# One matmul a unit later, and one load a tile later, in a two-layer attention kernel

## The chip, the cores and the metric

The kernel runs on one core of a Trainium2 chip. The metric is the device time of one execution in microseconds; the time before is 2504.33 us, the median of 3 runs (2504.14 to 2504.37). All arrays are f32.

A core has engines that run side by side, each through its own list of instructions in order, and that wait for one another by semaphores: TensorE (PE) multiplies matrices into PSUM, VectorE (DVE), ScalarE (ACT) and GpSimd (POOL) work elementwise, and SyncE (SP) issues most DMAs here.

## The reference

Four images of 128 channels by 64x64 pixels, so 4 batches of 4096 tokens of 128 channels, go through two layers. Cut to what matters:

```python
# layer 0: group norm, attention over all 4096 tokens, residual
xn = gn(x); q = Wq xn + bq; k = Wk xn + bk; v = Wv xn + bv      # q, k: 64 channels
x = x + v softmax(q^T k)^T
# layer 1: layer norm, causal attention with 128 channels, residual
t = tokens(x); n = ln(t)
t = t + softmax(mask(n Wq^T (n Wk^T)^T / sqrt(128))) (n Wv^T)
# recurrent feed-forward: layer norm, matrix, batch norm over all tokens, residual
w = bn(ln(t) W^T); y_i = sigmoid(w_i + y_{i-1} V^T); t = t + y
```

## The kernel before, in words

Work is cut into tiles of 512 queries (c = 0 to 7), in order of batch (b), layer, tile. A tile runs through its keys in units (u) of 2 x 128 keys: 16 units for each tile of layer 0, 2(c+1) units for tile c of layer 1, which is causal. The main loop emits, for each unit i, `score(i)`, one `step()` of side work, and `product(i-1)`.

`score` multiplies keys with queries into PSUM (L1090 in layer 0, L1083 in layer 1; tile `ps`) and ScalarE takes the exponential into `s`, one of three buffers (L1092, L1096). In layer 1 GpSimd masks the blocks on the diagonal (L1099). `product` adds `s` into `total` on VectorE (L1126, L1131) and multiplies it with the values into `av` in PSUM (L1134). In layer 1 the "values" are the normalised tokens themselves; the matrix of values W1v is applied to the finished tile instead.

When a tile has seen its last unit, a generator `finish` is made, and each `step()` advances it by one `yield`: VectorE sums `total` (L949 to L953), makes the reciprocal of the row sums (L957 to L964), and scales `av` to `o` (L966). Then `project` follows. In layer 0 it adds `o` to X (L975) and ends. In layer 1 it lets a number of steps pass (`waits`), multiplies `o` with W1v on TensorE (`po`, L981) and adds it to X, which gives `X2` (L984). When it is done, the feed-forward's part for this tile (`ffn`) enters the list of side work: the tile is stored (`kept`), turned to tokens by a transpose on VectorE (L758), a write to DRAM and four reads back (L760, L765, all on SP), and its statistics are taken (L740).

The side work beside layer 1 includes the keys of the next batch's layer 0: `xg` (normalised input, L681, after which GpSimd adds a bias to X, L683), `pk` (L686), `K` (L707, L708), and the values `pv` (L715, ScalarE's copy L716). In batch 0 these have no earlier layer to hide beside and run in the first tile of layer 0: the keys of block k are needed by unit 2k.

`load_x(b)` issues eight DMAs of 256 KB for one batch's input, on SP. For batch 1 it is called in `product`, with a small tile of `total` as `behind`: GpSimd first writes one column of each eighth of X from it (L505), and the DMAs, which overwrite those, wait for that. The statistics of batch 1 (`gn_stats`, L649: eight of 512 columns, then L653) are put into the side work when tile 2 of layer 0 begins. The order of instructions on each engine is not quite the order of emission: a scheduler with its own estimate of times sets it, except in stretches marked `manual_schedule`.

Of the kernel before, what the change touches and what calls it, by code (L numbers as in the profile page):

```python
# [32 lines left out]
QT = 512  # L33
# [441 lines left out]
def fast_kernel(  # L475
# [12 lines left out]
    NQ = N // QT  # L488
# [12 lines left out]
    def load_x(b, behind=None):  # L501

        X[b] = xpool.tile([P, N], F32, tag=f"X{b % 2}", name=f"X{b}")
        if behind is not None:
            nc.gpsimd.tensor_copy(X[b].rearrange("p (h n) -> p h n", h=8)[:, :, 0], behind)  # L505
        for h in range(8):
            eng = nc.scalar if b == 0 and h % 2 else nc.sync
            eng.dma_start(out=X[b][:, ts(h, N // 8)], in_=x[b, :, ts(h, N // 8)])
# [87 lines left out]
    with ExitStack() as actx:  # L596
# [10 lines left out]
        def misc(name):  # L607
            return ps_m.tile([P, QT], F32, tag="m", name=name)
# [335 lines left out]
        def finish(b, layer, c, off, w, av, total):  # L944

            name = f"{layer}_{b}_{c}_{off}"
            k = w // 32
            t = tmp.tile([P, QT], F32, tag="a", name=f"t_{name}")[:, :w]
            nc.vector.tensor_tensor(t, total[:, 0, :w], total[:, 1, :w], ALU.add)  # L949
            tt = tmp.tile([P, QT], F32, tag="b", name=f"tt_{name}")[:, :w]  # L950
            nc.vector.transpose(tt, t)  # L951
            part = small.tile([P, 16], F32, tag="part", name=f"part_{name}")
            nc.vector.tensor_reduce(part[:, :k], tt.rearrange("p (k j) -> p k j", j=32), AX.X, ALU.add)  # L953
            yield
            side = small.tile([32, 4, 16], F32, tag="side", name=f"side_{name}")
            for q in range(4):
                nc.vector.tensor_copy(side[:, q, :k], part[ds(32 * q, 32), :k])  # L957
            z = small.tile([P, 16], F32, tag="z", name=f"z_{name}")
            nc.vector.tensor_reduce(z[0:32, :k], side[:, :, :k].rearrange("j q k -> j k q"), AX.X, ALU.add)
            nc.vector.reciprocal(z[0:32, :k], z[0:32, :k])  # L960
            for q in range(1, 4):
                nc.vector.tensor_copy(z[ds(32 * q, 32), :k], z[0:32, :k])
            rb = tmp.tile([P, 16, 32], F32, tag="a", name=f"rb_{name}")[:, :k, :]
            nc.vector.transpose(rb, z[:, :k].unsqueeze(2).to_broadcast([P, k, 32]))  # L964
            o = tmp.tile([P, QT], F32, tag="b", name=f"o_{name}")[:, :w]
            nc.vector.scalar_tensor_tensor(  # L966
                o, rb.rearrange("p k j -> p (k j)"), GUARD, av[:, :w], ALU.mult, ALU.mult
            )
            yield from project(b, layer, c, off, w, o, 5 if w < QT else 3 if c == NQ - 1 else 2)

        def project(b, layer, c, off, w, o, waits):
            cols = ds(c * QT + off, w)
            xt = X[b][:, cols]
            if layer == 0:
                nc.vector.scalar_tensor_tensor(xt, o, 1.0 / GUARD, xt, ALU.mult, ALU.add)  # L975
                yield
                return
            for _ in range(waits):
                yield
            po = misc(f"po_{b}_{c}_{off}")[:, :w]  # L980
            nc.tensor.matmul(po, lhsT=W1v, rhs=o, start=True, stop=True)  # L981
            if c == 0:
                X2[b] = xpool.tile([P, N], F32, tag="X2", name=f"X2_{b}")
            nc.vector.scalar_tensor_tensor(X2[b][:, cols], po, 1.0 / GUARD, xt, ALU.mult, ALU.add)  # L984
            yield
# [17 lines left out]
        def whole(key):  # L1003
            for _ in made[key]:
                pass
            done(key)
# [98 lines left out]
        def product(i):  # L1105
            b, layer, c, off, w, u, n = units[i]
            d = st[b, layer, c, off]
            s, first = scores.pop(i)
            if u == 0:
                d["av"] = ps_av.tile([P, QT], F32, tag="av", name=f"av_{i}")  # L1110
                d["total"] = acc.tile([P, 2, QT], F32, tag="total", name=f"total_{i}")
            av, total = d["av"], d["total"]
            both = first[0] == first[-1]
            last = i == len(units) - 1
            if last:

                pz = misc("pz_last")
                for h in range(2):
                    nc.tensor.matmul(pz[:, 0:1], lhsT=total[:, h, :w], rhs=ones[:, 0:1], start=h == 0, stop=False)
            halves = (slice(0, len(first)),) if both else range(2)  # L1120
            if u == 0:
                if not both:
                    nc.vector.memset(total[:, 1, : first[1]], 0.0)
                for h in halves:
                    f = first[0] if both else first[h]
                    nc.vector.tensor_copy(total[:, h, f:w], s[:, h, f:w])  # L1126
            elif not last:
                for h in halves:
                    f = first[0] if both else first[h]
                    t = total[:, h, f:w]  # L1130
                    nc.vector.tensor_tensor(t, t, s[:, h, f:w], ALU.add)  # L1131
            V = V1[b] if layer else V0[b]
            for h in range(len(first)):
                nc.tensor.matmul(  # L1134
                    av[:, first[h] : w], lhsT=V[:, 2 * u + h, :], rhs=s[:, h, first[h] : w],
                    start=u == 0 and h == 0, stop=2 * u + h == n - 1,
                )
            if (b, layer, c, u) == (0, 0, 0, 4):
                load_x(1, total[:, 0, 0:8])
            if last:  # L1140
                for h in range(2):
                    nc.tensor.matmul(pz[:, 0:1], lhsT=s[:, h, :w], rhs=ones[:, 0:1], start=False, stop=h == 1)
                return av, pz, s
            if 2 * u + len(first) == n:
                for key in list(ends):
                    whole(key)
                key = ("e", b, layer, c, off, w)
                made[key] = finish(b, layer, c, off, w, av, total)
                ends.append(key)
# [25 lines left out]
        for i in range(len(units) + 1):  # L1175
            if i < len(units):
                score(i)
            if i:
                step()
                ended = product(i - 1)  # L1180
# [8 lines left out]
    with ExitStack() as fctx:  # L1189
# [94 lines left out]
        for n in range(1, len(steps[2])):  # L1284
# [15 lines left out]
            elif n >= last and late and WARM + late[0][1] + late[0][2] <= n:  # L1300
                b, l, k = late.pop(0)
# [76 lines left out]
```

## Time and profile before

| | |
|---|---|
| median of runs | 2504.33 us |
| the profiled execution: its time, its span | 2503.85 us, 2502.1 us |
| PE, DVE, ACT, POOL busy | 2466.4, 1778.1, 1137.5, 206.9 us |
| products `av`, layer 0 (L1134) | 2048 matmul instructions, 592 ns each with overlap |
| scores `ps`, layer 0 (L1090) | 2048, 492 ns |
| sums `total` (L1131) | 809 on VectorE, 882.5 us |
| granted TensorE clock | 0.998 |

In the profile's lines, a row of a group reads: line, engine, operation, output<-input, shape, count, then busy time and the mean of one. A row in order of time reads: start and duration in us, engine, line, operation, output<-input, shape and count, and in brackets the idle time of the engine before it and what ended it. A row of waits reads: who waited for whom, then total us, times, and the longest. Each f32 matmul of the program shows as two instructions, and matmuls overlap, so the distance from one start to the next says more than a duration.

### The profile page before, as it was taken

How to read it: one execution, taken by the hardware profiler on the slowest of the kernel's cores; microseconds unless marked ns; L12 is line 12 of the kernel's file. 1: busy time of each engine (PE TensorE's matmuls, PEld its weight loads, DVE VectorE, ACT ScalarE, POOL GpSimd, SP SyncE). 2: the span in 40 equal slices, each digit the busy share in tenths (PEclk: the TensorE clock that was granted, in tenths of full speed). 3: DMA queues.
4: the chain of work that ended last, by engine and by line, in shares of the span. 5: the costliest groups of instructions: out<-in, count | busy, mean ns of one | idle time of the engine just before them, and what ended most of it. 6: DMA issues, size and time to landing. Idle time of an engine off the chain costs nothing.

```text
span 2502.1 us, 22482 instructions
## 1 busy us (share of the span) xinstructions
PE 2466.4 (99%) x7345; PEld 1339.4 (54%) x7345; DVE 1778.1 (71%) x3571; ACT 1137.5 (45%) x1422; POOL 206.9 (8%) x281
## 2 busy tenths in 40 slices
PE   7999999999999999999999999999999999999997
PEld 4555554444555555444555555544455555544465
DVE  7776669655977667856687676876578676786667
ACT  4444444454444444445444444454444444434456
POOL 2010001210000100110000010121010000010000
PEclk9999999999999999999999999999999999999999
DMA  2000001100100000100010000101010000010023
GB/s 75 9 17 9 17 9 41 27 17 13 51 13 9 17 9 18 39 25 13 22 46 13 13 9 18 34 26 26 13 47 17 9 14 12 9 34 17 9 74 138
DMA packets 154078, 64.40 MB, mean 26 GB/s; under 512 B 136160, under 2 KB 136928, under 8 KB 152160
## 3 DMA queue, kind: packets, MB, share of 16 engines
q1 hardware_dynamic: 151344, 59.27, 8.9%
q10 hardware_dynamic: 2608, 3.61, 0.4%
q8 instruction: 60, 0.98, 0.2%
q14 instruction: 66, 0.54, 0.1%
HBM read 31.66 MB, written 31.20 MB: 25 GB/s over the span
## 4 chain that ended last, share of the span: by engine, by line
PE 94%; DVE 3%; ACT 2%; issue 1%; POOL 0%; DVEq 0%; POOLq 0%; ACTq 0%
PE av L1134 52%; PE ps L1090 19%; PE ps L1083 17%; PE po L981 1%; PE pw_f L841 1%; PE pq L804 1%; PE pv L715 1%; PE pk L686 1%; ACT WX L1234 1%; DVE total L1131 1%; ACT states L1234 0%; PE pz L1233 0%; ACT WXp L1234 0%; ACT s L1092 0%; DVE stats L649 0%
## 5 line engine op out<-in xcount | busy, mean ns | idle before, releaser
L1131 DVE TENSOR_TENSOR total<-total,s 128x1024 f32<-128x1024 f32 (+5 forms) x809 | 882.5, 1094 | 539.6 <-ACT s L1092 290.9
L1134 PE MATMUL av<-s,WXp 128*128 128x512 f32 x2048 | 962.1, 592 | 0.0
L1092 ACT ACTIVATE s<-ps,shift 128x1024 f32<-128x1024 f32 x512 | 569.6, 1114 | 760.4 <-PE ps L1090 743.5
L1090 PE MATMUL ps<-q,K 128*128 128x512 f32 x2048 | 757.5, 492 | 1.7 <-DVE K L708 1.5
L1096 ACT ACTIVATE s<-ps,zero,R 128x512 f32<-128x512 f32 (+3 forms) x607 | 405.3, 718 | 513.6 <-PE ps L1083 506.5
L1134 PEld LDWEIGHTS av<-s,WXp 128*128 128x128 f32 x2048 | 384.7, 188 | 303.6 <-issue 263.1
L1090 PEld LDWEIGHTS ps<-q,K 128*128 128x128 f32 x2048 | 386.0, 189 | 290.4 <-issue 230.7
L1134 PE MATMUL av<-s,V 128*128 128x512 f32 (+3 forms) x1214 | 504.3, 538 | 0.0
L1083 PE MATMUL ps<-q,X 128*128 128x512 f32 (+3 forms) x1214 | 503.5, 537 | 0.0
L1083 PEld LDWEIGHTS ps<-q,X 128*128 128x128 f32 x1214 | 225.1, 190 | 236.1 <-issue 219.4
L1134 PEld LDWEIGHTS av<-s,V 128*128 128x128 f32 x1214 | 223.9, 190 | 229.2 <-issue 205.7
L579 POOL TENSOR_TENSOR rstd<-rstd,mhalf 128x4 f32<-128x4 f32 x32 | 32.4, 1011 | 1024.2 <-DVE rstd L578 1024.2
L1099 POOL TENSOR_SCALAR_AFFINE_SELECT s<-s 128x128 f32<-128x128 f32 x128 | 49.0, 387 | 532.8 <-ACT s L1096 531.7
L579 POOL TENSOR_TENSOR rstd_f<-rstd_f,mhalf 128x4 f32<-128x4 f32 (+1 forms) x32 | 47.3, 1480 | 383.1 <-DVE rstd_f L578 362.6
L683 POOL TENSOR_SCALAR X<-X,B0v 128x512 f32<-128x512 f32 x32 | 64.5, 2019 | 139.8 <-DVE xg L681 138.3
L796 DVE TENSOR_SCALAR V<-V,lmv,rstd 128x128 f32<-128x128 f32 x128 | 38.6, 344 | 37.0 <-POOL rstd L579 36.9
L729 DVE TENSOR_TENSOR q<-QR,qh 64x512 fp32r<-64x512 f32 x64 | 44.0, 688 | 6.8 <-PE ps L1090 5.5
L949 DVE TENSOR_TENSOR t<-total 128x512 f32<-128x512 f32 x64 | 44.0, 688 | 4.3 <-PE pfw L638 2.5
L951 DVE STREAM_TRANSPOSE tt<-t 128x512 f32<-128x512 f32 x64 | 45.2, 706 | 1.8
L964 DVE STREAM_TRANSPOSE rb<-z 128x512 f32<-128x512 f32 x64 | 44.8, 700 | 0.9
L966 DVE SCALAR_TENSOR_TENSOR o<-rb,av 128x512 f32<-128x512 f32 x64 | 43.6, 681 | 2.4
L957 DVE COPY side<-part 32x16 f32<-32x16 f32 (+1 forms) x256 | 41.3, 161 | 3.9
(191 smaller groups left out, 1227.8 us busy)
## 6 DMA issues: line engine op xcount, KB each, us to landing
turn<-t SPq DMA_DIRECT2D x32, 256.0 KB, 2.0
V<-turn SPq DMA_DIRECT2D x128, 64.0 KB, 2.5
turn_f<-t_f SPq DMA_DIRECT2D x31, 256.0 KB, 2.0
t_f<-turn_f SPq DMA_DIRECT2D x124, 64.0 KB, 2.5
X<-in_x SPq DMA_DIRECT2D x28, 256.0 KB, 4.5
kept<-X SPq DMA_DIRECT2D x24, 256.0 KB, 2.0
Y<-kept SPq DMA_DIRECT2D x6, 1024.0 KB, 8.3
out<-Y SPq DMA_DIRECT2D x5, 1024.0 KB, 6.0
```

Source lines behind the costliest of these rows:

```text
L579: nc.gpsimd.tensor_tensor(dst, dst, mhalf[:, :n], ALU.pow)
L683: nc.gpsimd.tensor_scalar(xt, xt, B0v, None, ALU.add)
L729: nc.vector.tensor_tensor(q[ds((1 - h) * CQ, CQ), h, :], src, high[rows, :], ALU.subtract)
L951: nc.vector.transpose(tt, t)
L964: nc.vector.transpose(rb, z[:, :k].unsqueeze(2).to_broadcast([P, k, 32]))
L1083: nc.tensor.matmul(ps[:, h, first[h] : w], lhsT=lhsT, rhs=q[:, off + first[h] : off + w], start=True, stop=True,)
L1090: nc.tensor.matmul(ps[:, h, :], lhsT=lhsT, rhs=q[:, k, :], start=k == 0, stop=k == 1)
L1092: nc.scalar.activation(s, ps, AF.Exp, bias=shift)
L1096: nc.scalar.activation(part, ps[:, h, first[h] : w], AF.Exp, scale=scale, bias=zero)
L1099: nc.gpsimd.affine_select(out=edge, in_=edge, pattern=[[1, P]], base=0, channel_multiplier=-1, compare_op=ALU.is_ge, fill=0.0,)
L1131: nc.vector.tensor_tensor(t, t, s[:, h, f:w], ALU.add)
L1134: nc.tensor.matmul(av[:, first[h] : w], lhsT=V[:, 2 * u + h, :], rhs=s[:, h, first[h] : w], start=u == 0 and h == 0, stop=2 * u + h == n - 1,)
```

## The change

```diff
@@ finish
-            yield from project(b, layer, c, off, w, o, 5 if w < QT else 3 if c == NQ - 1 else 2)
+            yield from project(b, layer, c, off, w, o, 5 if w < QT else 3 if c in (1, NQ - 1) else 2)
@@ product
-            if (b, layer, c, u) == (0, 0, 0, 4):
+            if (b, layer, c, u) == (0, 0, 1, 4):
                 load_x(1, total[:, 0, 0:8])
```

The first edit lets one more step pass before `po` of tile 1 of layer 1, in each of the four batches. That tile's ending runs during tile 2, which has six units. The second edit calls the load of batch 1 sixteen units later, in tile 1 of layer 0 instead of tile 0. The statistics of batch 1 are still put into the side work at tile 2. Shapes, sizes and the number of matmuls and DMAs stay.

## The prediction

> **What bounds the kernel now.** I read the busy shares first, then the waits of TensorE, then its instructions in order of time at the two places that the change touches.
>
> ```profile
> span 2502.1 us, 22482 instructions
> PE 2466.4 (99%) x7345; PEld 1339.4 (54%) x7345; DVE 1778.1 (71%) x3571; ACT 1137.5 (45%) x1422; POOL 206.9 (8%) x281
> ```
>
> PE is busy for 99% of the span. The change adds and removes no matmul, so it can move the time only through gaps on PE. The waits of PE:
>
> ```profile
> PE pg L657 <- DVE mv L653: 10.6, 1, 10.6
> PE rest L1326 <- DVE good L1324: 5.1, 1, 5.1
> PE po L981 <- DVE o L966: 2.2, 3, 0.7
> PE pk L686 <- DVE xg L681: 1.7, 1, 1.7
> PE ps L1090 <- DVE K L708: 1.5, 3, 0.6
> ```
>
> 10.6 is the first load and 5.1 the closing check; the change touches neither, nor the 1.7 before the first keys. Left are `po` (2.2 us, three times) and `ps` behind `K` (1.5, three times). The ends of matmuls are modelled, so I measure both from start to start. First `po`, in batch 0:
>
> ```profile
> 404.75 1.88 PE L1134 MATMUL av<-s,V 128*128 128x512 f32 x4
> 406.47 1.67 PE L1083 MATMUL ps<-q,X 128*128 128x512 f32 x4
> 408.88 1.12 PE L981 MATMUL po<-o,W1v 128*128 128x512 f32 x2 [0.74 <-DVE o L966]
> 409.84 1.05 PE L715 MATMUL pv<-W0v,xg 128*128 128x128 f32 x8
> ```
>
> The same group of four scores (two 512, two 384 wide) took 1.50 us at 385.85. It therefore ended at 407.97, but `po` began at 408.88: 0.91 lost. From `po` to `pv` it is 0.96, against 0.86 for the unstalled `po` at 393.80: 0.10 more. In batch 1 (score group at 1008.04, `po` at 1010.43) the loss is 0.89+0.10, in batch 2 (1609.58, 1611.99) 0.91+0.11; the `po` of batch 3 at 2197.3 has no key matmuls around it and waits for nothing. Sum 3.0 us.
>
> The second place is the first tile, with two units to each block of 512 keys:
>
> ```profile
> 46.08 1.88 PE L1134 MATMUL av<-s,WXp 128*128 128x512 f32 x4
> 48.55 2.09 PE L1090 MATMUL ps<-q,K 128*128 128x512 f32 x8 [0.59 <-DVE K L708]
> ...
> 53.94 1.88 PE L1134 MATMUL av<-s,WXp 128*128 128x512 f32 x4
> 56.10 2.08 PE L1090 MATMUL ps<-q,K 128*128 128x512 f32 x8 [0.28 <-DVE K L708]
> ```
>
> Four `av` passes take 1.72 us (58.88 to 60.60, a turn without a wait), so `ps` could have begun at 47.80 and 55.66: lost 0.75 and 0.44. Likewise 0.20 before 40.69 and 0.31 before 70.55, nothing before 63.07. Sum 1.7 us. Why `K` is late, on VectorE:
>
> ```profile
> 58.45 2.56 DVE L1131 TENSOR_TENSOR total<-total,s 128x1024 f32<-128x1024 f32 x2 [2.50 <-ACT s L1092]
> 61.02 0.74 DVE L697 TENSOR_SCALAR QR<-pk,B0qk 64x512 f32<-64x512 f32 x1
> 61.78 0.42 DVE L707 TENSOR_SCALAR kh<-k 64x512 int32<-64x512 int32 x1
> 62.24 0.69 DVE L708 TENSOR_TENSOR K<-k,kh 64x512 fp32r<-64x512 f32 x1
> ```
>
> This is an undisturbed turn: K ends at 62.93 and `ps` starts at 63.07 (0.14 later), just in time. In the turns before, the eight L649 statistics of batch 1 (5.1 us of VectorE between 20 and 72) stand in this queue. All that PE can still win here is 3.0+1.7 = 4.7 us.
>
> [...] `pv` waited at 409.84 behind `po` with its own input long there. [...] beside batch 2's load a turn's write at 647.46 was read back only from 651.64 (4.2 us; at 94.38 it took 2.0). [...] the statistics here take 0.66 to 0.70 us with a load beside them or without.
>
> **The change, part by part.** I use the order of instructions on each engine that the built kernel has.
>
> 1. `po` of the second tile goes behind `pv` (8 passes, 0.89), the next `av` (1.72) and the narrow scores (0.65). PE then asks for `o` at 407.97+3.26 = 411.2; `o` began at 408.14 and took 0.69, so it is 2.4 us early. Gain 0.91+0.10 in each of three batches: **-3.0**. What is late next: X2 (L984) now waits for `po` at 412.1 instead of 409.8 and, in VectorE's queue, for the narrow sum of a GpSimd-masked score. That mask stands behind GpSimd's 1.57 us on X; xg at about 412.5 gives the masked score at 415.2, while PE wants it for `av` at 416.2: 1.0 us to spare. X2 then comes near 416, the transpose near 417.3 (414.49 before), its turn is back near 424, and its statistics stand behind a sum near 428. The FFN's own DMAs (one kept copy, one write, four reads on SP) move with it by under 3 us and nothing else waits on SP there. Cost 0; without that cover I would price the wait at 1.0 us a batch.
>
> 2. In the first tile the eight statistics and their aggregate (8 x 0.64 + 0.37 = 5.5 us of VectorE) leave. But the order on PE moves too: for four pairs the even unit's `ps` now stands before the last `av` product, 0.86 us earlier, and the odd one after it. I work out that loop. From the even `ps` (0) the odd one starts at 0.93+0.86 = 1.79; its exponential 1.21 later (83.11 to 84.32), 3.00, ends 4.11; the sum (1.23) ends 5.34; QR to the end of K 1.91 (61.02 to 62.93) and 0.14 to PE: 7.40. PE's own work in a turn is 1.86+0.86+1.72+0.89+1.72 = 7.05. So K is still 0.35 late in a turn. The first such `ps`: without the statistic of 0.69, K ends at 39.81, start 39.95. Three turns of 7.40 give 62.15; the last pair, not split, is PE's: 62.15+7.05+0.86 = 70.06, against 70.55. Gain **-0.5**. Ends: -1.7 if every wait goes, +0.5 if each of four turns loses 0.25 more than I count.
>
> 3. In the second tile the load's mark on GpSimd comes after the sum at 88.62 to 89.85; SP issues at 90.2 (0.2 after, as at 35.35 to 35.58) and eight issues of 0.43 end at 93.9, ahead of the turn's transpose. GpSimd is idle from 57 to 106 and SP from 39 to 94, so nothing is queued there. VectorE reaches the first statistic after X at 93.65; the first piece lands about 4.2 after its issue (646.13 to 650.32), 94.4: a wait of 0.8. With statistics and transpose between them, the sums of the next units end up to 2.7 us late. That is covered: three score buffers and 2.65 us a unit mean that a sum may be 7.94-1.11-1.23 = 5.6 us late before an exponential waits. The turn's write at 95 shares the engines with the load (36 to 43.3 before, so until 98), is read back near 104, and its reader, now behind another sum, comes at 107.8. Cost 0. A precedent is batch 2's load:
>
> ```profile
> 647.50 1.23 DVE L1131 TENSOR_TENSOR total<-total,s 128x1024 f32<-128x1024 f32 x1
> 650.32 1.36 DVE L649 BATCH_NORM_STATS2 stats<-X 128x6 f32<-128x512 f32 x2 [1.58 <-DMA X<-in_x]
> ```
>
> VectorE stood 1.58 us there and the scores on PE went on at 647.47, 650.12 and 652.76, one unit of 2.65 apart.
>
> Sum -3.0-0.5 = -3.5. The profiled execution took 2503.85 (span 2502.1 and 1.75 around it), so 2500.35; the median of runs is 0.48 above it: **2500.8 us**. Measurement tells about 0.2% (5.0 us) from no change, so this counts as same.
>
> **Rivals.** (a) All waits go: K is in time because VectorE runs ahead. For it: 63.07 shows a turn without loss; against it: the earlier `ps`. 2504.33-4.7 = 2499.6. (b) The first tile gains nothing or loses up to 0.5, as the earlier `ps` waits as long as the statistics did: 2501.3 to 2501.8. (c) `po`'s wait only moves: the masked score or a PSUM buffer holds PE 1.0 us in each batch. Against it: the 1.0 us to spare and the two buffers concerned, freed by q at 401.8 and by X2 at 400.6. 2503.8. (d) Slower: VectorE, in order, stands before the first statistic until the load lands, and sums and score buffers behind it stop ScalarE and then PE. It costs from a landing 2.9 us later than I count (5.6-2.7), 1 us for 1 us, and decides from 6.4 us, where it eats the 3.5; 8.5 us would be needed beyond that start for +5.0. Pieces landed within 6.7 us of issue, 2.5 later than 4.2, so it does not begin. A landing 9 us later gives 6.1-3.5 = +2.6, 2507. That the edit moves nothing is excluded by the built order for (1) and (2).
>
> **How the numbers follow.** My forecast 0.60, (a) 0.12, (b) 0.14, (c) 0.07, (d) 0.07. Range: the forecast with the ends of step 2 is 2499.6 to 2501.8; to leave out no more than 2 in 10 and allow for part of (c), 2499.4 to 2502.8. Faster than 2499.3 would need more than all the waits I found: 0.04. Slower by over 5.0 is the worse part of (d): 0.05. Same 0.91.
>
> **What would show it.** Right: no `po` in the list of PE's waits; `pv` directly after the 384-wide scores; no wait of 0.7 at any `ps` in the first tile, small ones of 0.3 at most; VectorE waiting about 1 us for X in the second tile; units 2.65 us apart there. Wrong: a new wait of PE on GpSimd's masked score near 415, units stretched between 90 and 110, or `K` waits as large as before.

## The result, and the profile after

The changed kernel takes 2500.82 us (median of 22 runs, 2500.48 to 2501.77); the kernel before took 2504.70 beside it (2503.66 to 2505.83). The ratio is 0.9985, with a 95% interval of 0.9979 to 0.9990: 3.9 us, or 0.16%. The interval lies below 1, but the difference is smaller than the 0.2% up to which it counts as no change. Where 3.9 us went can't be read from run times; the traces have to say it. The page of the changed kernel (profiled execution 2500.77 us):

```profile
span 2499.0 us, 22485 instructions
PE 2465.6 (99%) x7345; PEld 1338.1 (54%) x7345; DVE 1777.2 (71%) x3571; ACT 1137.3 (46%) x1422; POOL 211.3 (8%) x281
```

The same 7345 matmuls, and the span is 3.1 us shorter. Its waits of PE (who waited for whom, total us, times, longest):

```profile
PE pg L657 <- DVE mv L653: 10.7, 1, 10.7
PE rest L1326 <- DVE good L1324: 5.2, 1, 5.2
PE pk L686 <- DVE xg L681: 1.7, 1, 1.7
PE ps L1090 <- DVE K L708: 1.4, 4, 0.7
```

The line of `po` is gone; that of `K` stays almost as it was (1.4 against 1.5; one wait of each list, 0.7 here and 0.6 before, belongs to the very first keys, near 20 us, which the change doesn't touch). PE in order of time around `po` in batch 0:

```profile
406.42 1.67 PE L1083 MATMUL ps<-q,X 128*128 128x512 f32 x4
407.93 1.05 PE L715 MATMUL pv<-W0v,xg 128*128 128x128 f32 x8
408.82 1.88 PE L1134 MATMUL av<-s,V 128*128 128x512 f32 x4
410.54 0.82 PE L1083 MATMUL ps<-q,X 128*128 128x256 f32 x4
411.19 1.02 PE L981 MATMUL po<-o,W1v 128*128 128x512 f32 x2
```

The score group starts at 406.42, and 1.51 later `pv` follows, which is that group's own 1.50. `po` comes at 411.19, and the next row is 0.86 behind it. No stall is left. In the first tile, on PE:

```profile
46.29 1.02 PE L1134 MATMUL av<-s,WXp 128*128 128x512 f32 x2
47.52 1.17 PE L1090 MATMUL ps<-q,K 128*128 128x512 f32 x4 [0.21 <-DVE K L708]
...
53.78 1.02 PE L1134 MATMUL av<-s,WXp 128*128 128x512 f32 x2
55.01 1.16 PE L1090 MATMUL ps<-q,K 128*128 128x512 f32 x4 [0.21 <-DVE K L708]
```

Two `av` passes are 0.86 from start to start, so `ps` could have begun at 47.15 and 54.64: 0.37 lost in each turn, and a turn is 55.01-47.52 = 7.49. VectorE in one of those turns:

```profile
44.23 1.23 DVE L1131 TENSOR_TENSOR total<-total,s 128x1024 f32<-128x1024 f32 x1 [0.56 <-ACT s L1092]
45.47 0.74 DVE L697 TENSOR_SCALAR QR<-pk,B0qk 64x512 f32<-64x512 f32 x1
46.23 0.42 DVE L707 TENSOR_SCALAR kh<-k 64x512 int32<-64x512 int32 x1
46.69 0.69 DVE L708 TENSOR_TENSOR K<-k,kh 64x512 fp32r<-64x512 f32 x1
```

No statistic stands here any more, and still `K` is late: the chain sum, `QR`, `kh`, `K` starts from an exponential that ends at 44.2. In the second tile, where the statistics are now:

```profile
92.87 0.68 DVE L975 SCALAR_TENSOR_TENSOR X<-o,X 128x512 f32<-128x512 f32 x1
93.47 0.69 DVE L649 BATCH_NORM_STATS2 stats<-X 128x6 f32<-128x512 f32 x1
...
95.79 1.28 DVE L649 BATCH_NORM_STATS2 stats<-X 128x6 f32<-128x512 f32 x2
```

VectorE did not wait for the load at all (no bracket), and between 72 and 114 us PE is busy for 42.00 of 42 us, before and after.

### The profile page after: what moved, and what is told of

It reads as the page before. It is cut to its first block, busy times and chain, and to the rows that moved or that the text cites. A ratio compares the mean times of both kernels' runs of the same rounds, so it can differ in the third digit from the quotient of the medians.

```text
span 2499.0 us, 22485 instructions
## 1 busy us (share of the span) xinstructions
PE 2465.6 (99%) x7345; PEld 1338.1 (54%) x7345; DVE 1777.2 (71%) x3571; ACT 1137.3 (46%) x1422; POOL 211.3 (8%) x281
## 4 chain that ended last, share of the span: by engine, by line
PE 96%; ACT 2%; DVE 1%; issue 1%; POOL 0%; ACTq 0%; POOLq 0%; DVEq 0%
PE av L1134 53%; PE ps L1090 19%; PE ps L1083 18%; PE pq L804 1%; PE po L981 1%; PE pw_f L841 1%; PE pk L686 1%; PE pv L715 1%; ACT WX L1234 1%; ACT states L1234 0%; PE pz L1233 0%; ACT WXp L1234 0%; DVE total L1131 0%; PE rest L1254 0%; ACT s L1092 0%
```

## The experiments

The account at this point was: 3.0 us from `po`, the rest from the first tile. The rivals were that the wait of `po` moves on, that the load's own traffic rather than VectorE's statistics slows the first tile, and that the second tile isn't free. One thing was odd from the start: the profiles differ by 3.1 us and the runs by 3.9.

**The two edits apart.** The whole change once more, and each edit alone, on one chip (the kernel before: 2504.77, 57 runs).

> The changed kernel itself, run beside the two single edits so that all of them share one chip and one set of runs of the kernel before. By the prediction -3.5 us against before (2500.8 against 2504.3): -3.0 from the product with layer 1's values and -0.5 from the first tile. The two profiles taken so far differ by 3.1 us in their spans, the run times by 3.9.

Measured: 2500.83 us, ratio 0.9984 (0.9978 to 0.9991).

```diff
 # the product alone: the load stays
-            if (b, layer, c, u) == (0, 0, 1, 4):
+            if (b, layer, c, u) == (0, 0, 0, 4):
```

> The later product alone; the load stays in the first tile. My account: -3.0 us against before, the whole of the three stalls ahead of the product, and the first tile's key waits as in the kernel before (stalls of 0.20, 0.76, 0.44 and 0.31). If the load's move is worth more than I said, this kernel is 3.0 faster and the changed kernel 3.9 or more; if the wait ahead of the product had only moved on to the turn's chain, this kernel is at most 0.7 us faster.

Measured: 2501.18 us, ratio 0.9987 (0.9979 to 0.9995), so -3.6.

```diff
 # the load alone: the product stays
-            ... 3 if c in (1, NQ - 1) else 2)
+            ... 3 if c == NQ - 1 else 2)
```

> The load's move alone; the product stays two units after the last exponential. My account after the profile: -0.3 us against before (-0.5 as predicted), three stalls of 0.9 to 1.0 us ahead of the product as in the kernel before, key waits of 0.27 to 0.37 in each of the first tile's four turns. The rival that all key waits go with VectorE's statistics gives -1.7. If the 0.8 us by which the run times differ more than the spans belongs to the load, this kernel is about 1.1 us faster.

Measured: 2504.04 us, ratio 0.9998 (0.9989 to 1.0006), so -0.7 by the medians, with an interval that holds no change too. Neither the 0.3 of the account nor the rival's 1.7 is met. Its waits of PE:

```profile
PE po L981 <- DVE o L966: 2.4, 3, 0.9
PE pk L686 <- DVE xg L681: 1.7, 1, 1.7
PE ps L1090 <- DVE K L708: 1.6, 4, 0.9
```

`po` waits three times as before, so this edit leaves the stalls of the other alone. By the medians the two edits add up to 4.3 us, and together they gave 3.9; run times don't separate the two. To see what each is worth I cut every trace at one point, the first `av` of the second tile (78.50 us in the profile of before). The first column is from PE's first instruction to there, the second from there to PE's last; the first load, which comes before, varies by itself (in the profiles of all these runs PE begins at 10.45 to 10.93).

| kernel | first tile | the rest |
|---|---|---|
| before | 67.94 | 2412.94 |
| before, a second profile (below) | 68.86 | 2413.02 |
| product alone | 68.29 | 2409.97 |
| load alone | 67.72 | 2413.12 |
| both (the changed kernel's first profile) | 67.73 | 2409.95 |

The rest drops by 3.0 us in each kernel with the later product and in no other. The first tile is the same 67.7 in both kernels with the moved load; without it, it is another in each profile, from 67.94 to 68.86. A spread of 0.9 is enough for the 0.8 by which runs and profiles disagree.

**What varies in the first tile.** The kernel before, profiled again.

> The kernel before once more, unaltered, for a second profile. Its 57 runs have spans from 2502.3 to 2503.9 us (median 2503.0), all above the 2502.1 of the profile that I worked from, while the changed kernel's profile lies at its median. If that is the reason why the runs differ by 3.9 us and the spans of the two profiles by 3.1, this profile has about 0.9 us more of PE's waits than the first, and they stand in the first tile (key waits of 2 to 2.6 us in sum instead of 1.7) with the three waits ahead of the product at 3.0 as before. Rival: the three waits ahead of the product are what varies (3.0 to 3.9 in sum), and my 3.0 was measured on a short run.

Measured: 2504.84 us, span 2503.1, 1.0 us longer; the three waits of `po` are the same, and the wait for `K` ahead of the score that started at 48.55 (here at 49.44) is 1.66 us in place of the 0.75 that a start-to-start reading gives in the first profile. This execution lies 0.5 above the median of the same kernel on its chip (2504.30, 52 runs) and the first profile 0.5 below that of its runs, so neither is the typical one. The queue of VectorE there, in this second profile:

```profile
41.02 0.69 DVE L649 BATCH_NORM_STATS2 stats<-X 128x6 f32<-128x512 f32 x1
41.95 0.70 DVE L649 BATCH_NORM_STATS2 stats<-X 128x6 f32<-128x512 f32 x1 [0.24 <-DMA X<-in_x]
43.01 1.39 DVE L649 BATCH_NORM_STATS2 stats<-X 128x6 f32<-128x512 f32 x2 [0.37 <-DMA X<-in_x]
44.31 1.21 DVE L1131 TENSOR_TENSOR total<-total,s 128x1024 f32<-128x1024 f32 x1
```

In the first profile of before, which I predicted from, the same stretch reads:

```profile
41.04 2.47 DVE L649 BATCH_NORM_STATS2 stats<-X 128x6 f32<-128x512 f32 x4
43.42 1.21 DVE L1131 TENSOR_TENSOR total<-total,s 128x1024 f32<-128x1024 f32 x1
```

There the four statistics run back to back; here VectorE stands before them until pieces of the load land, and the sum behind them is 0.89 us later. `K`, and with it PE, is later by the same 0.89. The profile of the product alone lies between: its four statistics took 2.78 instead of 2.47 (+0.31), and its wait for `K` is 1.07 instead of 0.75 (+0.32). The load's issues, with KB and the median us from issue to landing, are first before, then the second profile of before:

```profile
X<-in_x SPq DMA_DIRECT2D x8, 256.0 KB, 4.5
```

```profile
X<-in_x SPq DMA_DIRECT2D x8, 256.0 KB, 6.2
```

The same eight transfers, issued at the same time, landed 1.7 us later in the median (between 39 and 41 us they moved 160 GB/s against 328). So one more thing than statistics stood in the first tile: their wait for the load, 0 to 0.9 us in three profiles. Why one execution moves less in those 2 us stays open.

**Statistics or traffic.** The load back in the first tile, the statistics held in the second.

```diff
-            if (b, layer, c, u) == (0, 0, 1, 4):
+            if (b, layer, c, u) == (0, 0, 0, 4):
                 load_x(1, total[:, 0, 0:8])
+            if (b, layer, c, u) == (0, 0, 1, 4):   # the tile that the statistics write
+                held[1] = small.tile([P, NQ, 6], F32, tag="stats", name="stats_1")
+                nc.gpsimd.tensor_copy(held[1][:, :, 0], total[:, 0, 0:8])
 ...   # left out: gn_stats(1) takes held[1] as the tile that it writes
```

> The later product, the load left in the first tile, and only the eight statistics of batch 1 held back to the second tile (GpSimd writes a column of their tile from the running sum there; the values that they give are the same). Order on PE as in the changed kernel. If the statistics on VectorE are what the load's move takes out of the first tile, this kernel equals the changed one: 2500.8 us within 0.2, key waits of 0.27 to 0.37 in the first tile. If the load's own traffic is what slows the first tile, it equals the kernel with the later product alone, 2501.2, or lies above it.

Measured: 2501.27 us (before on that chip 2504.30, ratio 0.9988, 0.9981 to 0.9994). That chip had no run of the changed kernel, so both were taken on one chip:

> The later product, load in the first tile, statistics in the second, once more beside the changed kernel on one chip; the first time it stood at 2501.27 on a chip without it. In its profile the waits of the first tile are those of the changed kernel, so by the account that the statistics and not the traffic cost the time it equals the changed kernel within 0.2. If the traffic in the first tile costs something that its profile did not show, it is 0.4 slower again.

> The changed kernel on the chip of the three runs beside it, as their base. The kernel before took 2504.77 us on one chip and 2504.30 on the other, so the base has to be on the same chip. Expected 2500.8, within 0.3.

Measured: 2500.68 with the held statistics, 2500.56 for the changed kernel, 0.12 apart, and first tiles of 67.79 and 67.71. The load's traffic costs the first tile no more than 0.1 us; the statistics in VectorE's queue, and what they wait for, cost it the rest.

**The query's add moved to ScalarE.** This takes 0.74 us out of the chain to `K`.

```diff
-                if b:
+                if b or c:
                     nc.scalar.activation(rows, pk[low, :], AF.Identity, bias=B0qk[low, :])
```

> The changed kernel, with the queries' bias add of batch 0's later tiles on ScalarE instead of VectorE, where it stands (0.74 us) between the two casts of the score and the key that the first tile's score product waits for. My account (what still makes the key late in the first tile is VectorE's queue of about four operations a turn): the key comes some 0.7 us earlier than it is wanted, so the 1.4 us of stalls left in the first tile go: -1.0 to -1.4 us against the changed kernel. Rival: ScalarE, which makes the key's add, the query's add and the exponentials in one queue, hands on the key later, and the stalls stay or grow: 0 to +1.5 us.

Measured: 2500.99 us, nothing gained, and neither account holds. ScalarE isn't late. On PE:

```profile
46.49 1.16 PE L1090 MATMUL ps<-q,K 128*128 128x512 f32 x4 [0.33 <-DVE K L708]
47.49 1.88 PE L1134 MATMUL av<-s,WXp 128*128 128x512 f32 x4
48.80 1.49 PE L1090 MATMUL ps<-q,K 128*128 128x512 f32 x4
```

The scheduler has put the even unit's score ahead of both passes of the `av` before it, not of one. So four `av` instructions now stand between the two scores of a block, not two, and the second exponential, from which the chain to the next `K` starts, comes 50.39-47.69 = 2.70 us after the first instead of 50.79-48.94 = 1.85 in the changed kernel. The 0.85 eats the 0.74; a turn is 7.60 against 7.48. That an earlier `K` is why the scheduler chose this order is a reading of the two orders; no run shows its reasons.

**The order alone.** The changed kernel, with the product emitted ahead of a block's first score.

```diff
+            late = 0 < i < 16 and i % 2 == 0
-            if i < len(units):
+            if i < len(units) and not late:
                 score(i)
             if i:
                 step()
                 ended = product(i - 1)
+            if late:
+                score(i)
```

> The changed kernel with another order of emission in the first tile alone: ahead of each block's first score the product of the unit before is emitted. On PE the two score groups of a block then stand together, behind all four products (ps, ps, pk, av, av, pv), instead of one inside the products. My account: a turn is then 0.93 (odd score) + 1.21 + 1.11 (exponential) + 1.23 (sum) + 1.85 (query, high part, key) + 0.14 = 6.5 us for the key, against 7.05 of PE's own work, so the key waits go: -1.4 us against the changed kernel, about 2499.4, with turns of 7.05 instead of 7.48. Rival: VectorE's queue has more in it than I count and the key comes late there too: no gain, or a loss of up to 1 us.

Measured: 2499.62 us, ratio 0.9981 (0.9974 to 0.9989), span 2497.6. On PE:

```profile
46.69 1.05 PE L715 MATMUL pv<-W0v,xg 128*128 128x128 f32 x8
47.50 2.10 PE L1090 MATMUL ps<-q,K 128*128 128x512 f32 x8
...
53.73 1.05 PE L715 MATMUL pv<-W0v,xg 128*128 128x128 f32 x8
54.54 2.10 PE L1090 MATMUL ps<-q,K 128*128 128x512 f32 x8
```

No bracket, a turn of 7.04, and a first tile of 66.30, which is 1.42 below the changed kernel's. The runs agree: on the same chip the kernel with held statistics (2501.27) and the one in the next experiment (2501.10), whose traces in the first tile are the changed kernel's within 0.1, took 1.5 to 1.7 more. This is the fastest version found. With the scores of a block together, as the kernel before had them from 40.69 on (the products stand in another order than there), the waits for `K` go in every turn but the last: from `pv` to the last block's score, at 69.00, it is 1.21 instead of 0.81, so 0.40 is still lost. Whether this order would give as much with the load left in the first tile was not run.

**Two units later.** `po` of the second tile with `waits` of 4.

> The changed kernel with the product of the second tile in layer 1 two units later instead of one. If one unit already takes away the whole wait and what hangs on X2 (transpose, its turn through DRAM, statistics) is covered, this kernel equals the changed one: 2500.8 within 0.3. If the 0.34 us that the masked score has to spare, or the turn's chain, is used up by the longer delay, a new wait of PE of 0.5 to 1 us comes in each of three batches: +1.5 to +3 us.

Measured: 2501.10 us (before on that chip 2504.30, ratio 0.9987, 0.9981 to 0.9994). The rest of its trace is 2409.98 us, the same as with one unit. X2 comes at 418.12 instead of 415.98, and nothing on PE waits for it: one unit took the whole wait, and the chain behind has at least 2 us more.

**How late VectorE may be in the second tile.** Extra operations on VectorE behind the statistics.

```diff
+            if (b, layer, c, u) == (0, 0, 1, 9):
+                for _ in range(8):                 # and 16
+                    nc.vector.tensor_scalar(total, total, 1.0, None, ALU.mult)
```

> The changed kernel with eight more operations on VectorE (the running sum times 1, 128x1024, in place; values unchanged) behind the statistics in the second tile of layer 0, at about 104 us: some 8 x 0.69 = 5.5 us by the statistics' own rate per element and instruction, to be read from its trace. By the prediction's cover (three score buffers: a sum may be 5.6 us late before an exponential waits) it costs nothing: 0 to 0.5 us against the changed kernel. Rival, that VectorE's lateness reaches PE as it is: +5.5.

> The same with sixteen operations, twice the time on VectorE (11 us at the estimate). By the cover of 5.6 us, and about 1.3 that PE's product has behind the exponential, PE loses 11 - 5.6 - 1.3 to 11 - 5.6, so +4 to +5.5 us, if the operation takes 0.69. With another duration d it is 16 d - 6.9 to 16 d - 5.6, which must hold for the run with eight too (0 where negative). Rival: all 16 d.

Measured on the chip where the changed kernel took 2500.56: 2501.79 with eight (+1.2) and 2509.41 with sixteen (+8.9). One operation takes 0.69 for 1024 elements a row, and a statistic 0.68 for 512: the expectation's figure was met, though not by a statistic's rate per element. With eight, the sum that starts at 103.73 in the changed kernel comes here on VectorE:

```profile
109.50 1.21 DVE L1131 TENSOR_TENSOR total<-total,s 128x1024 f32<-128x1024 f32 x1
```

and on ScalarE the exponential that needs its buffer:

```profile
107.97 1.11 ACT L1092 ACTIVATE s<-ps,shift 128x1024 f32<-128x1024 f32 x1 [1.53 <-PE ps L1090]
...
110.81 1.11 ACT L1092 ACTIVATE s<-ps,shift 128x1024 f32<-128x1024 f32 x1 [1.72 <-DVE total L1131]
```

The sum is 5.7 us late (this trace as a whole runs 0.09 later than the changed kernel's), and the exponential, due at 107.97+2.65 = 110.62, is 0.19 late: the cover is about 5.5 us, close to the 5.6 that was worked out. On PE the `av` groups stay 2.65 apart (110.42, 113.07), so the 0.19 is hidden too. What the eight cost is elsewhere: at 135.27, where PE waits 0.65 us (0.81 from start to start) for `dev`, which VectorE makes in the group norm of batch 1 and which is late with it; the rest of the trace is 2410.85 us, 0.9 more. With sixteen, PE in the list of waits and in slices of 1 us (span of the slice, busy times, granted clock, DMA):

```profile
PE av L1134 <- ACT s L1092: 6.1, 1, 6.1
```

```profile
120.00:121.00 1.00, 1.00 (x2) 0.48 (x2) 1.00 (x2) 0.95 (x1) 0.00 (x0) 0.50 0.06 16
121.00:122.00 1.00, 1.00 (x2) 0.37 (x2) 0.94 (x4) 0.00 (x0) 0.00 (x0) 0.50 0.00 0
```

The sum starts at 117.19, 13.1 late (this trace runs 0.34 later as a whole) and not 11.0, because the scheduler placed the statistics and the normalisation of the turned tile among the operations. That less 5.5 and 1.3 gives 6.3; PE lost 6.2. On top of it PE ran at a granted clock of 0.50 afterwards: four `av` and the next score took 4.44 us (119.67 to 124.11) instead of 2.65, 1.8 more. So the formula of the expectation held for the wait (with the measured 13.1 in place of 16 d). It missed the clock with sixteen operations, and with eight the later wait for `dev`.

## Why the prediction was right, and where it was not

**Step 1, `po`: right, mechanism and size.** -3.0 was counted from three stalls; the part of the trace behind the first tile is shorter by 2412.94-2409.95 = 2.99 us. `po` came at 411.19 (411.2 said) and X2 at 415.98 (416). One detail was thinner than said: the masked score was to have 1.0 us to spare and had 0.34. GpSimd's operation on X, which the mask stands behind, now meets VectorE's sums:

```profile
412.96 2.32 POOL L683 TENSOR_SCALAR X<-X,B0v 128x512 f32<-128x512 f32 x1 [3.14 <-DVE xg L681]
```

In the profile of before it was 1.57 us (414.68 to 416.25, VectorE idle from 415.20 on). Here 0.97 us of it fall where VectorE adds `s` to `total` (412.78 to 413.93), and it takes 0.75 us more; VectorE's two sums take 1.15 us, as they did in the profile of before without GpSimd beside them. In other rows of the changed kernel's trace it takes 1.56 with VectorE idle (from 40.57) and 2.61 beside a sum of 1.25 (from 467.51). What makes it longer beside a sum is not shown. Rival (c) needed this chain to hold PE up; even with two units, where X2 comes 2.1 us later still, it doesn't.

**Step 2, the first tile: the mechanism right, the size wrong in two ways.** The term of 7.40 for a turn, with K "still 0.35 late", measured 7.48, since the odd unit's exponential comes 0.05 and the end of its sum 0.08 later in a turn than in my chain; after three turns and the last pair the gain against the profile that I worked from was 67.94-67.73 = 0.2, not 0.5. That was one error. (In the list of waits for `K`, 0.60 of the 1.5 is the first keys' at 19.71; the prediction's sum of 1.7 was counted from starts and doesn't hold it.) The other was to take that profile for the typical one. Its statistics never waited for the load; in the second profile they did, and `K` with them, so that the first tile's gain there is 68.86-67.73 = 1.1. In the runs the load's move is worth 0.7 alone and 0.35 beside the later product (2501.18 against 2500.83). The prediction foresaw such a wait of VectorE in the new place, where it costs nothing and didn't come, and did not look for it in the old place, where it is on the path.

**The base: an error that made up for it.** The sum was made against the profiled execution and 0.48 us was added, by which the median of runs stood above it, as if both kernels had it. The changed kernel's profile (2500.77) lies at the median of its runs (2500.82), without the 0.48. The load's wait, which the change removes, is the likely reason, but it isn't shown for those runs, and the ends of the span vary as well: another profile of the changed kernel took 2501.30 with the same first tile and the same rest (67.72 and 2409.93). With both terms mended the sum is 2503.85-3.0-0.2 = 2500.6. That the forecast of 2500.8 met 2500.82 so closely is thus luck: its terms don't deserve it.

**Step 3, the second tile: right.** The cost is 0, and the cover, worked out as 5.6 us, was measured as about 5.5. The first piece landed within 3.4 us of its issue and not 4.2, so VectorE didn't wait the 0.8; the sums were up to 1.0 us late (102.22 against 101.34 before, in a trace that runs 0.06 earlier as a whole) instead of 2.7, and the turn was read back at 99.64 instead of near 104 (4.84 us after its write was issued, against 2.02 in the profile of before; from 92 to 98 us the DMA engines were busy for 0.96 of the time). Rival (d) would have needed the sums some 4.5 us later still. The run with sixteen operations shows what that costs: its sum outran the cover by 7.6 us, and the trace behind the first tile grew by 7.9, as the half clock added somewhat more than PE's product hid.

**Rivals (a) and (b).** Rival (a), that all waits for `K` go, was turned down because of the earlier `ps`, and rightly so for this kernel; the run with the other order comes near it, with one wait of 0.40 left and 2499.6 as worked out for (a). So the order of the scores cost the changed kernel about 1.4 us. Rival (b), that the first tile gains nothing, was near: 0.2 gained in the profile, 0.35 to 0.7 by the medians of runs.

What stays open: the product alone is 3.6 us faster in the runs (13 of them, spans 2499.1 to 2500.7), 0.6 more than its place in the trace gives. Its first tile waits for the load as before, and 0.6 is within the 0.9 that this wait varied by in three profiles; it was not separated further. For the same reason the part of the load's move stands only as 0.2 to 1.1 us in traces.

## What to carry to other kernels

An engine that waits for a transfer in order makes what stands behind it as uncertain as the transfer: here a sum, `K` and PE were all late by the same 0.89 us. Look for that wait where the transfer stands now, too, and profile the kernel before more than once where less than 1 us matters. And when an input gets earlier, ask what a scheduler will do with it: here the consumer moved forward too, in an order that made the next producer later, and 1.4 us of gain only came when the order was held.

## What the runs showed of the hardware

In the run with sixteen operations PE's last matmul before the wait ended, by its modelled end, at 113.59 and the next began at 119.67. The granted clock was 1.00 from 112 to 114, 0.50 from 119 to 123, 0.94 from 123 to 124 and 1.00 from 124 to 126, so it rose near 123.1, 3.4 us after that matmul began. The fall lies between: from the mean of 0.92 over 95 to 140 us I estimate 115.5 to 116.4, which is 1.9 to 2.8 us after the modelled end. Behind the longest wait for `K` (1.66 us, 47.4 to 52 us in the second profile of before) the clock stayed at 1.00. PE's wait with sixteen operations, 6.2 us, thus cost 8.0, with the 1.8 at half clock. GpSimd's 128x512 operation on X took 1.56 us with VectorE idle and up to 2.85 beside its sums (32 of them in the changed kernel's trace), and the eight transfers of 256 KB landed in a median of 4.5 or 6.2 us in two profiles of the same kernel.
